# A decoder layer on one core: five row buffers, single part buffers, larger DMA pieces and a new order

## The chip, the cores and the metric

The kernel runs on one core of a Trainium2 chip. The metric is the device time of one execution in microseconds; lower is better. Before the change, three runs gave 1161.72, 1155.21 and 1157.89 us, so the median is 1157.89 us.

## The reference

The reference is one pre-norm decoder layer on `x` (16 batches, 256 rows, 512 columns, float32) with a context of the same shape. It has three steps, each added to `x`:

```python
x = x + attn(layernorm(x), q_w, q_b, k_w, k_b, v_w, v_b, o_w, o_b)   # 16 heads of 32, causal softmax
x = x + xattn(ctx, ctx, layernorm(x), ssm_kernel, D, 8)              # products k*v, long convolution, times q
x = x + ffn(layernorm(x), w_gate_up, w_down)                         # rows and weights rounded to 8 bits, SiLU gate
```

In the second step every pair of channels of a group of 8 is multiplied along the sequence, convolved with a kernel of 512 taps, and multiplied by the normalized `x`. In the third, rows and weights are quantized to 127 levels and scaled back, and the width between is 1408.

## The kernel before, in words

**Two stages.** Until about 622 us on the profile's clock the kernel works on attention, batch by batch; each batch has four units of four heads, 64 units in all. Beside this, GpSimd builds the products of context channels (the "pairs") and stores them in device memory, and the feed-forward weights are quantized. After that come 32 tiles of 128 rows, each with the convolution, the normalization and the feed-forward layer.

**The way of one batch through attention.** `norm_load` (L670) brings 256 rows of `x` into a buffer `xt`. VectorE takes the statistics (L679 to L681), GpSimd the inverse root (`norm_root`, L685), ScalarE writes the normalized rows `xn` (`norm_rows`, L696). For accuracy, rows and weights are each held as a sum of two float16 parts: `turn_hi` (L705, ScalarE) makes `xh`, `turn_lo` (L712, GpSimd) makes the rest `xl`. Two DMA transposes (`turn_out`, L718) turn them into `xhT` and `xlT`, which the query, key and value projections read (`mm3`, L658 to L660: three matmuls for each product). The buffer `xt` is still in use: GpSimd adds the output bias to it (`norm_bias`, L701), and at the end of the batch the output projection is added to it (`out_rows`, L745) and it is stored (`out_store`, L750, twice for each batch). Only then may the buffer take a new batch.

**The way of one unit.** The projections of queries and keys go from PSUM to `qkhl` in two parts each (`project_hi` L766, `project_lo` L771). `project_store` (L778) writes them to device memory, and five DMAs of `project_stack` (L785) read them back, stacked on 96 partitions, as `st`. Then come the scores (L800), the maximum (L809), the exponentials (L816), the inverse sums spread to 32 columns each in `lb` (`scores_spread`, L827, GpSimd), the transposes of the probabilities (L841) and the weighting with the values (`weigh_mm`, L869 to L876). There the inverse sums are transposed too and copied to `lt` (L882), and the result is scaled with them (L887).

**What sets the order.** The order on each engine is fixed before the run by a planner in the kernel's own code (class `Plan`). Every step has an engine, an expected duration, the steps that it follows, the buffers that it takes, and a due time. The planner goes through the steps on a clock of its own; of the steps that are ready and have room in their buffers, it takes the one with the earliest due time. Each engine then runs its instructions in that order, and so does the queue of SyncE (SP), which issues every DMA of the kernel: an instruction that waits holds up all behind it. The due times are formulas in T = 8.8 (the planner's length of a unit), with a table of shifts on top, one row for each kind of step and one column for each stretch of planned time:

```python
pl.add(("xi", b), "SP", t - 9.5 * T, 0.44, norm_load, b, late=1.9, dma=1.5, new=[xt])
...
pl.add(("xp", b), "POOL", t - 8.3 * T, 0.69, norm_root, b, late=0.1, after=[("xs", b, 1)])
...
pl.add(("xh", b), "ACT", t - 7.5 * T, 0.94, turn_hi, b, after=[("xr", b, 0), ("xr", b, 1)], new=[("xh", b)], use=[("xn", b)])
...
s["when"] += v[sum(s["when"] >= b for b in bounds)] if v else 0.0
```

In the planner's keys, `xi` is the load of a batch, `xs` its statistics, `xp` the root, `xc` the shift, `xr` the normalized rows, `xh` and `xl` the two parts, `xo` the two transposes, `qm` the query and key projections, `xb` the bias, `pi` the load of a projection weight.

**The start.** The four projection weights (1 MB each) are loaded (L596), their squares are summed for a scale (`proj_norm`, L603), the scale goes through two small matmuls and a dozen small VectorE instructions (L608 to L639), and the weights are transposed on TensorE (`proj_turn`, L646) and split into two float16 parts (`proj_hi` L649, `proj_lo` L653).

Of the kernel before, what the change touches and what calls it, by code (L numbers as in the profile page):

```python
# [108 lines left out]
def kernel(  # L109
# [16 lines left out]
    P = 128  # L126
# [416 lines left out]
    if True:  # L543
# [50 lines left out]
        def proj_in(nm):  # L594
            wl = wld.tile([P, KC, D], F32, name=f"wl_{nm}")
            nc.sync.dma_start(wl, dict(q=q_w, k=k_w, v=v_w, o=o_w)[nm].rearrange("(o p) i -> p o i", p=P))  # L596
            wraw[nm] = wl
# [17 lines left out]
        def scale_top(j):  # L615
            pt, t2 = tps2[j]
            ti = t2.bitcast(I32)
            nc.vector.tensor_reduce(t2[:, 0:1], pt[:2, :P], op=ALU.max, axis=AX.X)
            nc.vector.tensor_scalar(t2[:, 0:1], t2[:, 0:1], 4.0, 2.0 ** -30, ALU.mult, ALU.max)

            nc.vector.tensor_scalar(ti[:, 1:2], ti[:, 0:1], 1, EXPMASK, ALU.logical_shift_right, ALU.bitwise_and)
            nc.vector.tensor_scalar(t2[:, 2:4], idf[:2, :2], t2[:, 1:2], None, ALU.mult)
# [5 lines left out]
        def scale_all(j):  # L628
# [8 lines left out]
            nc.vector.tensor_tensor(bias[:, j:j + 2, :], bias[:, j:j + 2, :], ap(sc, j, [[1, 2], [0, KC]]), ALU.mult)  # L637
# [9 lines left out]

        def proj_hi(nm, kc):
            nc.scalar.activation(wT[nm][0][:, kc, :], wps[nm, kc], AF.Copy, scale=sc[:, 2, names.index(nm):names.index(nm) + 1])  # L649

        def proj_lo(nm, kc):
            hi, lo = wT[nm]
            nc.vector.scalar_tensor_tensor(  # L653
                lo[:, kc, :], wps.pop((nm, kc)), sc[:, 2, names.index(nm):names.index(nm) + 1], hi[:, kc, :],
                ALU.mult, ALU.subtract)
# [9 lines left out]
        XB, STB = 3, 4  # L665


        def norm_load(b):
            xt = ap2.tile([P, 2, DX], F32, tag="xt", bufs=XB, name=f"xt{b}")
# [33 lines left out]
        def turn_hi(b):  # L703
            xh = ap2.tile([P, 2, D], F16, tag="xh", name=f"xh{b}")
# [4 lines left out]
        def turn_lo(b):  # L709
            xn, xh = xns.pop(b)  # L710
            xl = ap2.tile([P, 2, D], F16, tag="xl", name=f"xl{b}")
# [63 lines left out]
        def project_store(b, g):  # L775
            pjs.pop(("qk", b, g))
            qk_d = dram.tile([4, P, S], F16, tag="qk_d", bufs=4, name=f"qk_d{b}_{g}")
            nc.sync.dma_start(qk_d.rearrange("n p s -> p n s"), qks.pop((b, g)))  # L778
            qkd[b, g] = qk_d

        def project_stack(b, g, n):
            if n == 0:
                stks[b, g] = ap2.tile([96, 2, 4, S], F16, tag="st", bufs=STB, name=f"st{b}_{g}")
            r3, first, n, src = ((0, 0, 2, 1), (1, 0, 1, 1), (1, 1, 1, 3), (2, 0, 1, 0), (2, 1, 1, 2))[n]
            nc.sync.dma_start(  # L785
                stks[b, g][32 * r3:32 * r3 + 32].rearrange("r j h s -> r (j h) s")[:, 4 * first:4 * first + 4 * n, :],
                bass.AP(qkd[b, g].tensor, qkd[b, g].offset + src * P * S, [[S, 32], [32 * S, 4 * n], [1, S]]))


        def scores_mm(b, g, qc, h2):  # L790
# [8 lines left out]
            for hh in range(2):  # L799
                nc.tensor.matmul(  # L800
                    ps[:, hh, :nk], stk[:, 0, 2 * h2 + hh, qc * P:(qc + 1) * P], stk[:, 1, 2 * h2 + hh, :nk],
# [23 lines left out]
        def scores_spread(b, g):  # L825
            lb = ap2.tile([P, 2, P], F32, tag="lb", bufs=2, name=f"lb{b}_{g}")
# [53 lines left out]
        def weigh_sums(b, g):  # L880
            lt = ap2.tile([P, S], F32, tag="lt", name=f"lt{b}_{g}")
# [179 lines left out]
        def weight_scales_out():  # L1061
# [12 lines left out]
        pl = Plan(xt=XB, xn=1, xh=2, xl=2, xhT=2, xlT=2, v=2, pj=2, qk=3, st=STB, s=2, pr=2, lb=2, pt=3, tt=2, av=1,  # L1074
                  lt=2, ah=2, ct=1, cr=2, kT=2, p=2, kv=2, qw=3, qb=2, qt=2, x1=5, q=2, qT=4, sd=1, kv2=3, c=2, u=UB, oT=3, x2=8, xn2=2, xb=2, xq=5, ac=3,
# [5 lines left out]
        for n, nm in enumerate(names):  # L1081
            j = n // 2
            pl.add(("pi", nm), "SP", -80 + 10 * n, 0.55, proj_in, nm, late=1.5, dma=3.3)
# [73 lines left out]
        def batch(b):  # L1157
            t = KC * T * b
            xt = ("xt", b)
            if True:  # L1160
                pl.add(("xi", b), "SP", t - 9.5 * T, 0.44, norm_load, b, late=1.9, dma=1.5, new=[xt])
                if b == 0:
                    pl.add("ob", "SP", -45, 0.5, bias_rows, late=2.0, dma=0.8)
# [117 lines left out]
        for i in range(NT):  # L1281
# [76 lines left out]
        bounds = (60,330,570,680,1010)  # L1358
        shift = {
            ("bi", 2): (0.8, 5.7, 3, 5.9, 1.9, 8.6),  # L1360
            ("bk", 3): (14.4, 12.2, -4.6, 11.1, 15.6, 13.5),
            ("bn", 2): (-4.8, 0.7, 13.6, -2.3, -10.8, 2.5),
            ("bp", 2): (0.2, -9, 3.2, 0, 2.1, 3.1),
            ("bq", 2): (8.5, -3.6, 0.7, 0.7, -24, 0.7),
            ("br", 2): (6.5, 6.7, 1.5, 1.5, -20.1, 1.5),
            ("bs", 2): (0.5, 0.5, 12, 0.5, 20.5, 11.6),
            ("bt", 2): (-3.1, 4.5, 6, 10.4, -3.2, -23.3),
            ("ck", 2): (-1.3, -3.1, -0.1, 0.4, -3.2, -0.3),
            ("cl", 3): (-2.5, 1.1, -0.3, 2.3, -4.4, 1.3),
            ("cm", 2): (-3.9, -1.5, -4.7, -1, -1.5, -4.8),  # L1370
            ("cm", 3): (-3.3, -0.5, 5.2, 4.4, 7.2, -7.4),
            ("co", 2): (-2.8, 5.1, -9.1, 6.1, -12.9, -12.1),
            ("cr", 2): (-4.6, 3.8, -1.4, 0.3, 0.6, 8),
            ("cs", 3): (-7.5, -6, -24.7, -8.3, -15.4, -9.2),
            ("ct", 3): (2, 2.5, 0.3, 0.3, 5.3, -0.5),
            ("cu", 3): (0.2, 1.3, -10.5, -7.1, -6.1, 10.5),
            ("cw", 2): (-1.4, 14, 15.9, -13.5, -1.4, -10.2),
            ("cx", 2): (-27.7, -25.8, -20.3, 0.1, -26.2, -22.6),
            ("cz", 2): (-0.6, 1.6, 0.1, -1.1, 0.1, 0.1),
            ("dm", 2): (9.4, 21.8, 4.5, 11.7, 42.3, 23.4),  # L1380
            ("do", 2): (6.5, -0.8, -1, -6.8, -0.7, -20.7),
            ("dr", 2): (17.3, 17, 7.9, 9, 24.4, 14.2),
            ("ds", 2): (-1.2, -1.7, 7, -1.7, -3.6, 4.7),
            ("fc", 3): (-1.3, 2.5, -6.8, -2.3, 1.7, 1.8),
            ("fd", 2): (-0.3, 0.4, -7.3, 2.9, 0.4, -2.9),
            ("fm", 2): (-14, -14, -17.7, -12.3, -15.4, -10.3),
            ("fm", 3): (1.6, 0.8, -2.2, -0.7, 6.5, 3.9),
            ("fn", 2): (0.2, 0.9, -0.7, 0.2, 2, -4.5),
            ("fo", 2): (2.3, -7.2, 16.2, 3.2, 1.4, -7.2),
            ("fp", 2): (6.6, -2.6, 6.6, -1.9, -11, -3.8),  # L1390
            ("fq", 2): (0.8, -4.2, 0.7, -3, 5.5, 0.8),
            ("fr", 2): (-4.7, 2.6, -0.2, 8.5, 5.7, -28.6),
            ("fs", 2): (-0.1, -20.6, -16.5, 0.2, -23.3, -16.9),
            ("ft", 2): (0.6, 15.2, 12.5, 0.6, 7.1, -0.6),
            ("fv", 2): (1.4, -0, 2.3, -0.3, -8.8, 0.3),
            ("fw", 2): (-1.5, 12.8, 14.2, 14.4, 7.3, 13.3),
            ("gl", 3): (-0.4, 0.4, -0.4, -0.4, -1.3, 0.2),
            ("gm", 4): (0.2, 0.2, 0.4, -2.3, 0.8, -0.2),
            ("gs", 3): (5.5, -5.8, 4.4, 7.8, 8.9, 7.6),
            ("gu", 3): (0.5, 11.3, 16.5, 10.1, 0.5, 24.4),  # L1400
            ("om", 4): (1.9, -9, 5.4, 5.1, -0.8, 3.8),
            ("or", 3): (2.2, 12.8, -4, -0.4, -4, 2.9),
            ("os", 3): (-2.5, 6.4, 18.1, 4, 7.2, 14.8),
            ("pa", 2): (-0.2, 2.1, 1.2, -0.2, -0.2, 2.1),
            ("pb", 2): (8.6, -0.4, 4.8, 4.8, 5.7, 5.9),
            ("pc", 2): (-20.3, -17.7, 4.8, 0.4, 3.9, 4.8),
# [93 lines left out]
```

## Time and profile before

| | before |
|---|---|
| median of 3 runs | 1157.89 us (1155.21 to 1161.72) |
| the profiled execution | 1164.23 us, span 1162.4 us, mean granted TensorE clock 0.993 |
| TensorE busy | 1076.4 us (93%) |
| VectorE busy | 1015.8 us (87%) |
| GpSimd busy | 947.5 us (82%) |
| ScalarE busy | 838.0 us (72%) |
| DMA | 229.48 MB in 269026 packets, mean 197 GB/s |

All durations below come from the one profiled execution. A line such as L670 is a line of the kernel. A wait in the tables is idle time of the engine named first, put down to whatever released it last. SPq is the queue of SyncE. In the rows by window, each engine's busy time is followed by the number of its instructions, then come the granted TensorE clock (1.00 is full speed), the busy share of the 16 DMA engines, and GB/s.

### The profile page before, as it was taken

What the parts mean: (1) busy time and instruction counts of PE and PEld (TensorE: products, weight loads), DVE (VectorE), ACT (ScalarE), POOL (GpSimd) and SP (SyncE); (2) the same over time, 40 slices, a digit from 0 to 9 for tenths busy, and PEclk for the clock granted to TensorE, in tenths of its full rate; (3) what the DMA queues carried; (4) which work ended last, traced back from release to release, by engine and by line L of the source; (5) the groups of instructions that cost most, each with busy time, mean ns of one, the idle gap of its engine ahead of it and who ended that gap; (6) DMA issues with size and microseconds to landing.
All of it is one profiled execution on the core that took longest, in us unless ns stands there. A gap on an engine that the chain in (4) does not pass through costs nothing.

```text
span 1162.4 us, 25593 instructions
## 1 busy us (share of the span) xinstructions
PE 1076.4 (93%) x8503; PEld 766.8 (66%) x8503; DVE 1015.8 (87%) x3188; ACT 838.0 (72%) x1999; POOL 947.5 (82%) x924
## 2 busy tenths in 40 slices
PE   4999889999999989999999889999999999999965
PEld 3766657776667756776666666767767667766632
DVE  5999678888788877987787999999999999999997
ACT  6898878898998878998885456575556566655444
POOL 4497888889999966899514799999999999999962
PEclk9999999999999999999999999999999999999989
DMA  7687798888888977879548956657666766676422
GB/s 244 166 226 246 207 225 219 246 262 229 229 245 233 264 215 199 251 228 258 172 145 274 280 153 189 186 148 192 168 175 169 186 167 168 174 187 156 102 48 66
DMA packets 269026, 229.48 MB, mean 197 GB/s; under 512 B 125177, under 2 KB 223519, under 8 KB 268767
## 3 DMA queue, kind: packets, MB, share of 16 engines
q1 hardware_dynamic: 268895, 227.85, 70.4%
q8 instruction: 67, 1.10, 0.4%
q14 instruction: 64, 0.52, 0.1%
HBM read 124.10 MB, written 75.74 MB: 172 GB/s over the span
## 4 chain that ended last, share of the span: by engine, by line
DVE 32%; PE 31%; POOL 13%; ACT 9%; DMA 8%; issue 5%; SPq 2%; DVEq 0%; POOLq 0%; ACTq 0%
DVE hp L450 4%; PE g L425 4%; ACT p L816 3%; DVE s L454 3%; DVE u L338 3%; DVE p L809 3%; PE pj_qk L659 3%; PE pj_qk L658 3%; PE pj_qk L660 3%; DMA xlT<-xl 2%; DVE u L341 2%; PE c L324 2%; PE c L326 2%; PE c L325 2%; POOL g L443 2%
## 5 line engine op out<-in xcount | busy, mean ns | idle before, releaser
L816 ACT ACTIVATE p<-p,nmax 128x256 f32<-128x256 f32 (+1 forms) x512 | 230.0, 454 | 11.3 <-DVE nmax L809 10.7
L809 DVE CUSTOM_DVE_ANT_0 p<-s,mask,esc 128x128 f32<-128x128 f32 (+1 forms) x512 | 187.1, 411 | 14.8 <-PE s L800 14.6
L324 PE MATMUL c<-bkv,T 128*128 128x288 f16 x640 | 183.2, 286 | 9.4 <-issue 3.2
L325 PE MATMUL c<-bkv,T 128*128 128x288 f16 x640 | 183.1, 286 | 0.0
L326 PE MATMUL c<-bkv,T 128*128 128x288 f16 x640 | 183.0, 286 | 0.0
L425 PE MATMUL g<-w,xq 128*128 128x384 bf16 (+1 forms) x1024 | 169.1, 315 | 13.1 <-DVE o L528 6.3
L964 POOL TENSOR_TENSOR kv<-p,kv 128x1152 f16<-128x1152 f32 x64 | 152.0, 2382 | 7.9 <-ACT kv L959 7.8
L946 POOL TENSOR_TENSOR p<-kT 128x1024 f32<-128x1024 f32 x64 | 143.9, 2249 | 2.3
L425 PEld LDWEIGHTS <-xq 128*128 128x128 bf16 x1024 | 100.4, 98 | 68.0 <-issue 8.1
L443 POOL TENSOR_TENSOR g<-g,sw 128x704 f32<-128x704 f32 x60 | 101.0, 1705 | 3.9 <-ACT g L436 3.9
L816 ACT ACTIVATION_READ_ACCUMULATOR p<-p,nmax 128x1 f32 x512 | 100.4, 196 | 0.0
L800 PE MATMUL s<-st 96*128 96x128 f16 (+1 forms) x512 | 84.5, 247 | 8.9 <-DVE nmax L809 8.4
L338 DVE TENSOR_TENSOR u<-c,qT 128x512 f32<-128x512 f32 x128 | 87.3, 682 | 5.9 <-PE c L326 5.3
L766 ACT ACTIVATE qkhl<-pj_qk,bias 128x256 f16<-128x256 f32 x128 | 59.8, 469 | 45.3 <-PE pj_qk L660 33.7
L771 DVE SCALAR_TENSOR_TENSOR qkhl<-pj_qk,bias,qkhl 128x256 f16<-128x256 f32 x128 | 59.9, 478 | 33.5 <-ACT qkhl L766 21.0
L827 POOL TENSOR_SCALAR lb<-lsum 128x256 f32<-128x256 f32 x64 | 26.0, 406 | 75.6 <-DVE lsum L823 48.9
L357 POOL TENSOR_TENSOR u<-u 128x512 f32<-128x512 f32 x60 | 76.9, 1282 | 9.6 <-DVE u L338 9.6
L510 PE MATMUL d<-w,hq 128*128 128x512 bf16 x352 | 80.9, 379 | 3.8 <-DVE hp L450 3.0
L324 PEld LDWEIGHTS <-T 128*128 128x128 f16 x640 | 62.6, 98 | 29.1 <-DVE u L344 5.9
L659 PE MATMUL pj_qk<-xlT,wq_hi 128*128 128x256 f16 x256 | 70.5, 275 | 10.7 <-DMA xlT<-xl 10.7
L841 PE MATMUL pt<-idf,p 128*128 128x128 f32 x524 | 79.9, 275 | 0.0
L658 PE MATMUL pj_qk<-xhT,wk_hi 128*128 128x256 f16 x256 | 70.0, 273 | 7.3 <-ACT qkhl L766 6.9
(236 smaller groups left out, 3326.1 us busy)
## 6 DMA issues: line engine op xcount, KB each, us to landing
kv_d<-kv SPq DMA_DIRECT2D x64, 576.0 KB, 3.5
bkv<-kv_d SPq DMA_DIRECT2D x64, 576.0 KB, 3.9
qk_d<-qkhl SPq DMA_DIRECT2D x64, 256.0 KB, 2.9
st<-qk_d SPq DMA_DIRECT2D x256, 64.0 KB, 2.7
T<-pad_d SPq DMA_DIRECT2D x64, 256.0 KB, 4.2
x_d<-xt SPq DMA_DIRECT2D x32, 256.5 KB, 3.5
bx<-x_d SPq DMA_DIRECT2D x32, 256.5 KB, 3.6
xt<-in_x_dram SPq DMA_DIRECT2D x16, 512.0 KB, 4.2
```

Source lines behind the costliest of these rows:

```text
L324: nc.tensor.matmul(reg, T[:, 0, d:d + P], kv[:, mi, 0, :], start=mi == 0, stop=False)
L325: nc.tensor.matmul(reg, T[:, 0, d:d + P], kv[:, mi, 1, :], start=False, stop=False)
L326: nc.tensor.matmul(reg, T[:, 1, d:d + P], kv[:, mi, 0, :], start=False, stop=mi == li)
L338: nc.vector.tensor_tensor(ap(u, uo, [[UW, 2], [64, 4], [1, 64]]), ap(pc, 0, [[512, 2], [64, 4], [1, 64]]), ap(qT, qo, [[96, 2], [8, 4], [1 ...
L425: nc.tensor.matmul(pg[:, :c.stop - c.start].rearrange("p (r o) -> p r o", o=P), t["xq"][:, kc, :], w1[:, (o + c.start) // P:(o + c.stop) / ...
L443: (nc.gpsimd if i < NT - 2 else nc.vector).tensor_tensor(ts[i]["g1"][:, c], ts[i]["g1"][:, c], sw1[:, I + c.start:I + c.stop], ALU.mult)
L658: nc.tensor.matmul(ps, lh, rh, start=first, stop=False)
L659: nc.tensor.matmul(ps, lh, rl, start=False, stop=False)
L809: nc.vector.tensor_tensor_reduce(out=prs[b, g][qc][:, h, :], in0=ps[:, hh, :nk], in1=mask2[:, P - qc * P:2 * P], op0=ALU.add, op1=ALU.min, ...
L816: nc.scalar.activation(pr[:, h, :], pr[:, h, :], AF.Exp, scale=-1.0, bias=nmax[:, qc, h:h + 1], accum_out=lsum[:, qc, h:h + 1])
L946: nc.gpsimd.tensor_tensor(ap(p, 0, [[NKV, 4], [64, 4], [1, 64]]), ap(kT, o, [[96, 4], [0, 4], [1, 64]]), ap(kT, o, [[96, 4], [8, 4], [1, 6 ...
L964: nc.gpsimd.tensor_tensor(kv[:, :, 1, :], p, kv[:, :, 0, :], ALU.subtract)
```

## The change

It has five parts.

- The rows of a batch (`xt`) get five buffers in place of three, each a little narrower.
- The two float16 parts `xh` and `xl`, the spread inverse sums `lb` and their transposed copy `lt` get one buffer in place of two.
- Larger pieces: the projection weights are read so that a partition gets four whole consecutive rows (8 KB together) and not four rows that lie apart (2 KB each). The transposed columns then come out in another sequence, and `cols` puts them back as the two parts are written. The queries and keys are stored as 2 KB for each partition in place of four pieces of 512 B, and `st` has its axes swapped, so that one of the five reads moves pieces of 1 KB; the other four keep 512 B.
- Two small VectorE instructions of the scale become a `scalar_tensor_tensor`.
- The order: the load of the output weight may come only after the second transpose of batch 0, two planned durations differ, and every row of the table of shifts is new, with eight columns in place of six.

```diff
-            nc.sync.dma_start(wl, dict(q=q_w, k=k_w, v=v_w, o=o_w)[nm].rearrange("(o p) i -> p o i", p=P))
+            nc.sync.dma_start(wl, dict(q=q_w, k=k_w, v=v_w, o=o_w)[nm].rearrange("(p o) i -> p o i", p=P))
...
-            nc.vector.tensor_scalar(t2[:, 2:4], idf[:2, :2], t2[:, 1:2], None, ALU.mult)
+            nc.vector.scalar_tensor_tensor(t2[:, 2:4], idf[:2, :2], 1.0, ap(t2, 1, [[0, 2]]), ALU.mult, ALU.mult)
...
-            nc.vector.tensor_tensor(bias[:, j:j + 2, :], bias[:, j:j + 2, :], ap(sc, j, [[1, 2], [0, KC]]), ALU.mult)
+            nc.vector.scalar_tensor_tensor(bias[:, j:j + 2, :], bias[:, j:j + 2, :], 1.0, ap(sc, j, [[1, 2], [0, KC]]), ALU.mult, ALU.mult)
...
+        def cols(t):
+            return t.rearrange("k (p o) -> k o p", o=KC)
+
         def proj_hi(nm, kc):
-            nc.scalar.activation(wT[nm][0][:, kc, :], wps[nm, kc], AF.Copy, scale=sc[:, 2, names.index(nm):names.index(nm) + 1])
+            nc.scalar.activation(cols(wT[nm][0][:, kc, :]), wps[nm, kc].rearrange("k (o p) -> k o p", o=KC), AF.Copy,
+                                 scale=sc[:, 2, names.index(nm):names.index(nm) + 1])
...
-        XB, STB = 3, 4
+        XB, STB = 5, 4
...
-            xt = ap2.tile([P, 2, DX], F32, tag="xt", bufs=XB, name=f"xt{b}")
+            xt = ap2.tile([P, 2, D + 4], F32, tag="xt", bufs=XB, name=f"xt{b}")
...
-            xh = ap2.tile([P, 2, D], F16, tag="xh", name=f"xh{b}")
+            xh = ap2.tile([P, 2, D], F16, tag="xh", bufs=1, name=f"xh{b}")
...
-            xl = ap2.tile([P, 2, D], F16, tag="xl", name=f"xl{b}")
+            xl = ap2.tile([P, 2, D], F16, tag="xl", bufs=1, name=f"xl{b}")
...
-            qk_d = dram.tile([4, P, S], F16, tag="qk_d", bufs=4, name=f"qk_d{b}_{g}")
-            nc.sync.dma_start(qk_d.rearrange("n p s -> p n s"), qks.pop((b, g)))
+            qk_d = dram.tile([P, 4, S], F16, tag="qk_d", bufs=4, name=f"qk_d{b}_{g}")
+            nc.sync.dma_start(qk_d, qks.pop((b, g)))
...
-                stks[b, g] = ap2.tile([96, 2, 4, S], F16, tag="st", bufs=STB, name=f"st{b}_{g}")
-            r3, first, n, src = ((0, 0, 2, 1), (1, 0, 1, 1), (1, 1, 1, 3), (2, 0, 1, 0), (2, 1, 1, 2))[n]
+                stks[b, g] = ap2.tile([96, 4, 2, S], F16, tag="st", bufs=STB, name=f"st{b}_{g}")
+            r3, j, w, src = ((0, 0, 2, 1), (1, 0, 1, 1), (1, 1, 1, 3), (2, 0, 1, 0), (2, 1, 1, 2))[n]
             nc.sync.dma_start(
-                stks[b, g][32 * r3:32 * r3 + 32].rearrange("r j h s -> r (j h) s")[:, 4 * first:4 * first + 4 * n, :],
-                bass.AP(qkd[b, g].tensor, qkd[b, g].offset + src * P * S, [[S, 32], [32 * S, 4 * n], [1, S]]))
+                stks[b, g][32 * r3:32 * r3 + 32].rearrange("r h j s -> r h (j s)")[:, :, j * S:(j + w) * S],
+                bass.AP(qkd[b, g].tensor, qkd[b, g].offset + src * S, [[4 * S, 32], [32 * 4 * S, 4], [1, w * S]]))
...
-            lb = ap2.tile([P, 2, P], F32, tag="lb", bufs=2, name=f"lb{b}_{g}")
+            lb = ap2.tile([P, 2, P], F32, tag="lb", bufs=1, name=f"lb{b}_{g}")
...
-            lt = ap2.tile([P, S], F32, tag="lt", name=f"lt{b}_{g}")
+            lt = ap2.tile([P, S], F32, tag="lt", bufs=1, name=f"lt{b}_{g}")
...
-            pl.add(("pi", nm), "SP", -80 + 10 * n, 0.55, proj_in, nm, late=1.5, dma=3.3)
+            pl.add(("pi", nm), "SP", -80 + 10 * n, 0.55, proj_in, nm, late=1.5, dma=2.9, then=[("xo", 0, 1)] * (n == 3))
...
-                    pl.add("ob", "SP", -45, 0.5, bias_rows, late=2.0, dma=0.8)
+                    pl.add("ob", "SP", -45, 2.0, bias_rows, late=2.0, dma=0.8)
...
-        bounds = (60,330,570,680,1010)
+        bounds = (-50,10,60,330,570,680,1010)
...
-            ("qm", 3): (0, 1.9, -1.6, -1.4, -1.6, -1.4),
+            ("qm", 3): (1, -6.6, 5.6, 2.5, -4.1, 4.8, 6.6, -4.6),
...
-            ("xh", 2): (1, -0.1, -0.1, -0.1, 32.8, 1),
+            ("xh", 2): (47.7, 33.2, 30.1, 31.9, 36.7, 30.1, 35, 2.8),
-            ("xi", 2): (-29.5, 8.3, 8.2, -18.2, 5.6, -45.6),
+            ("xi", 2): (0, -12.5, 1, 5.4, 8.4, 4.4, -4.3, 6.3),
...
-            ("xo", 3): (-36.7, -30.1, 24.9, -48.9, -48.1, -40.2),
-            ("xp", 2): (-3.4, 1.4, -4, -3.5, -14.8, -3.3),
+            ("xo", 3): (-1.3, 9.6, -0.7, -20.2, -2.7, 0.3, 4.7, 9.5),
+            ("xp", 2): (37.9, 32.2, 44.8, 31.9, -0.9, 38.6, 34.4, 31.5),
...
```

The table has about ninety such rows; the ones shown are those of a batch's way to its projections.

## Prediction before the run

> **What bounds the kernel now.** I read the page's totals first, then busy time by window, then who waited for whom, and last the timeline around the longest of those waits. The totals, and the attention stage in four windows (the columns are named with the profile above):
>
> ```profile
> span 1162.4 us, 25593 instructions
> PE 1076.4 (93%) x8503; PEld 766.8 (66%) x8503; DVE 1015.8 (87%) x3188; ACT 838.0 (72%) x1999; POOL 947.5 (82%) x924
> ...
> 25.00:60.00 35.00, 33.36 (x279) 26.38 (x278) 31.32 (x117) 28.65 (x72) 16.19 (x15) 1.00 0.58 151
> 60.00:330.00 270.00, 253.70 (x2208) 183.59 (x2206) 227.61 (x871) 236.93 (x716) 236.70 (x191) 0.99 0.82 231
> 330.00:570.00 240.00, 224.82 (x1953) 161.70 (x1952) 193.48 (x752) 210.42 (x624) 210.09 (x167) 0.99 0.83 235
> 570.00:622.00 52.00, 49.61 (x451) 34.68 (x449) 43.45 (x166) 42.63 (x152) 7.15 (x13) 1.00 0.60 188
> ```
>
> TensorE carries attention: 561.5 of 597 us busy, so 35.5 us is the most that any order can win there. From 680 to 1100 us TensorE and VectorE are both above 95% busy; an edit before that moves this stage as a whole. What TensorE waited for in 60 to 620 us (total, times, longest), and two waits of the SP queue:
>
> ```profile
> PE pj_qk L659 <- DMA xlT<-xl: 10.7, 6, 3.7
> PE s L800 <- DVE nmax L809: 7.2, 16, 1.7
> PE pj_qk L658 <- ACT qkhl L766: 6.9, 9, 1.1
> ...
> SPq L785 <- DMA qk_d<-qkhl: 72.4, 41, 4.8
> ...
> SPq L670 <- DMA x_d<-xt: 21.0, 8, 6.2
> ```
>
> The first place is the late transpose of `xl`. The SP queue shows why: the load of `xt` waits for the store of the batch three before it. One case, from store to stall:
>
> ```profile
> 399.47 0.35 SPq L750 DMA_DIRECT2D x_d<-xt  x1
> ...
> 404.34 0.40 SPq L670 DMA_DIRECT2D xt<-in_x_dram  x1
> ...
> 423.06 1.32 SPq L718 DMA_TRANSPOSE xlT<-xl  x1
> ...
> 429.26 0.37 PE L659 MATMUL pj_qk<-xlT,wq_hi 128*128 128x256 f16 x1 [3.44 <-DMA xlT<-xl]
> ```
>
> Store, 4.9 us, load, 18.7 us, transpose, 6.2 us, matmul. All thirteen loads from batch 3 on are issued 2.9 to 6.6 us after a second store of the batch three before (108.08 after 104.19, 132.70 after 127.97, 180.07 after 175.91, and so on). The stall also costs clock (the granted clock is the third number from the right):
>
> ```profile
> 428.00:430.00 2.00, 0.74 (x4) 0.54 (x4) 1.76 (x2) 0.00 (x0) 0.00 (x0) 0.74 1.14 361
> 430.00:432.00 2.00, 2.00 (x12) 1.54 (x11) 0.17 (x2) 0.20 (x1) 0.00 (x0) 0.50 0.73 273
> 432.00:434.00 2.00, 2.00 (x18) 1.79 (x18) 0.73 (x2) 2.00 (x4) 0.00 (x0) 0.91 0.67 250
> ```
>
> The missing clock is (0.26 + 0.50 + 0.09) x 2 = 1.7 us. The stall at 161.73 (3.67 us) has 0.68, 0.50 and 0.97 behind it: 1.7 us too.
>
> **The change part by part.**
>
> *Five row buffers.* The load of batch b then waits for the store of batch b-5, two batches or about 70 us earlier, so the 18.7 us from load to transpose no longer follow a store. This takes away TensorE's 10.7 us and the 3.4 us of clock: -14.1 us. What is late next is `xh` and `xl` themselves if the order asks for them late (below). The load adds nothing to SP (0.38 us each, as many as before); SP also loses the 21.0 us for which all DMAs behind a blocked load stood still. Ends: 0 and, with what that freed queue gives the later waits, -18.
>
> *Single part buffers.* Here the Trainium skill ("Trainium Kernel Development and Optimization", Best Practices) speaks against the change: it says to double-buffer so that transfers lie beside computing. By that rule four rings lose their overlap. The trace: `xh` and `xl` are written 1.04 and 2.13 us long and are free once the transposes land, 3.9 and 3.5 us after issue; from batch 2 on the next batch's transposes come 26 us or more later. `lt` is read to its end at least 2.9 us before its next copy. Only `lb` is held: in this trace 12 of its 63 successors are written before the transposes at L869 have read the one before (taken as done 0.9 us before the copy at L882 starts), by 30.6 us together. But 1.0 us of this lies before 430 us, 4.1 us in the stall just shown, 0.5 us near 475, 9.6 us at 507 to 540 us, where GpSimd is full, and the other 15.4 us after 565 us, where it has little else to do. Its pairs end with the store at 572 us and are first read at 603.8 us: 30 us of cover. If that cover were gone, the 9.6 us would come on the path, and `xl`, queued behind a waiting `lb` on GpSimd, would hold TensorE. By the rule +10, by the trace 0; I take 0.
>
> *Larger pieces.* The skill's "DMA: Bandwidth & Descriptors" (Specifications) calls 512 B enough for full line rate, so pieces of 512 B and 2 KB have nothing to win: 0 us. The trace is less kind to small pieces: in 5 to 10 us, weights and rows in 2 KB pieces move 363 GB/s at a share of 0.99, while the window 140 to 160 us, with many 512 B and transposed pieces, moves 217 GB/s at 1.00. Yet what can be won is small: a store of 256 KB in 512 B pieces lands in 2.9 us, one of 576 KB in pieces of over 4 KB in 3.5 us, a read of 128 KB in 2.9 us and one of 64 KB in 2.7 us. At an estimated 0.3 us for each of 64 stores and 64 larger reads, SP and DMA win some 38 us in sum, but TensorE waited for `st` only 0.4 us in all. The scores are far behind their reads. I take 0 (-4 to +1). The axes of `st` change no matmul.
>
> *The start.* Of the first 25 us TensorE is busy 8.9. The chain goes weight q landing at 8.45, squares (1.91), rows and part of batch 0 (1.5 + 1.04), squares of k to 14.9, scale to 18.4, parts and transposes, first projection at 25.36. The k weight landed near 12.6, just when ScalarE came free, so faster pieces alone win at most 0.3 us; the new order can win the 2.5 us of rows on ScalarE. Moving the output weight's load (1 MB, issue 1.97 us) behind the second transpose (issued 16.25) spares it and costs nothing: its squares start at 25.33, its transposes at 36.3. The strided writes of 32 ScalarE and VectorE instructions (0.67 and 0.75 us) are not shown anywhere; the nearest row, the copy at L933 that writes in rows of 64, takes 0.577 us against 0.581 for a plain one, so 0, at worst doubled on the eight that stand before the first projection: +4. The two `scalar_tensor_tensor` are 0.22 and 0.17 us now; beside GpSimd a VectorE addition of one element a row (L981) took 1.68 us, so -1 to +2. I take -1 for the start (-3 to +5).
>
> *The rest of the order.* Every due time is new, so waits of 7.2 + 6.9 us and the losses between the stages (620 to 680 us: TensorE 7.7, VectorE 8.0 us idle) and in the last 60 us are dealt anew. Nothing in the trace gives a sign; 0, from -18 (half of these and the tail's) to +20.
>
> Sum: -14.1 - 1 = -15 us, that is 1149 against this execution's 1164.2 (span and 1.8 us around it). That execution lies 6.3 us above the median of the runs, so I set the sum against the median: 1157.9 - 15 = 1143 us.
>
> **The rivals.**
>
> *The idle time only moves.* Without the wait for `xlT`, TensorE meets the maximum (L809) or the parts of `qkhl` a little later: these two already cost 14.1 us, most of them under 1 us. For it: ScalarE is 88% busy in 60 to 570 us. Against: the two long stalls, 7.1 us and all of the lost clock, belong to no other engine. Then only some 3 us remain: 1155.
>
> *The new order also gathers the rest.* Idle time of 35.5 falls to 10, with the clock 3.4, the start 3, the transition 3: -35, 1123. For it: three columns of the table shape the time before 60 on the planner's clock, in place of one. Against: no order keeps TensorE at 98% with four engines above 80%.
>
> *The new order brings the wait back (slower).* The table puts the root (`xp`) and the part `xh` back by 30 to 48, while the projections (`qm`) move by at most 10. On the planner's scale `xh` was due 66 us ahead of its batch and is now due about 35; the projections are due about 30 ahead. Between lie `xh`, `xl`, a transpose and its landing: 1.04 + 2.13 + 1.3 + 3.5 = 8 us. If that chain slips as it did at 423 us, every batch stalls and not two. With 3.5 us of idle and 1.7 us of clock at every second of 13 batches, 34 us stand against the 14 won: +20, 1178. It decides from 1.1 us a batch on. Against: due times are only ranks among steps that are ready, and the rows now lie in SBUF long before.
>
> *The change doesn't do what it says:* five buffers do nothing if the planner still plans with three. It is given the same constant, `xt=XB`, so I leave this out.
>
> **How the numbers follow.** About 0.5% (5.8 us) is what a measurement of this kernel can tell from no change. The main forecast, 1132 to 1152, gets 0.48; the large gain 0.16; the idle time that moves 0.14, all of it within 0.5%; the slower case 0.22. So faster 0.64, same 0.14, slower 0.22. The range 1120 to 1168 leaves out the best third of the large gain and the worse half of the slow case.
>
> **What would show it.** Right: no wait of L670 on `x_d`, TensorE's wait for `xlT` under 2 us, no granted clock below 0.95 in 100 to 560 us, attention over near 607 us in place of 622, and 620 to the end as long as before. Wrong: a wait for `xlT` in most batches (slow rival); a first projection after 27 us (strided writes); GpSimd waiting before L827 with pairs stored after 595 us (`lb`); or a conv stage longer by over 6 us.

## The result, and the profile after

The kernel after takes 1165.02 us (median of 6 runs, 1163.77 to 1165.61), the one before 1158.47 us (6 runs): a ratio of 1.0055, with a 95% interval of 1.0035 to 1.0075. So it is 6.5 us slower, where 15 us faster was forecast. The profiled execution after took 1165.3 us. Lines of code lie 5 further down than before (L675 loads rows, L723 transposes, L791 reads `st`, L806 scores, L815 maximum). The totals, the start and the attention stage in the windows of before (start and end in us, length, busy time of TensorE, its weight loads, VectorE, ScalarE and GpSimd with counts, granted clock, DMA share, GB/s):

```profile
span 1163.5 us, 25635 instructions
PE 1077.3 (93%) x8503; PEld 765.7 (66%) x8503; DVE 1021.1 (88%) x3188; ACT 846.1 (73%) x1999; POOL 948.1 (81%) x924
...
0.00:25.00 25.00, 6.72 (x27) 5.16 (x28) 14.99 (x44) 16.13 (x17) 9.46 (x15) 1.00 0.88 304
25.00:60.00 35.00, 28.45 (x206) 21.33 (x205) 32.20 (x91) 30.46 (x58) 10.94 (x7) 1.00 0.44 119
60.00:330.00 270.00, 252.97 (x2192) 182.54 (x2191) 223.57 (x869) 237.46 (x703) 242.38 (x196) 0.98 0.82 232
330.00:570.00 240.00, 231.43 (x2044) 168.19 (x2042) 203.17 (x788) 214.65 (x658) 191.71 (x155) 1.00 0.79 229
570.00:622.00 52.00, 50.62 (x442) 34.85 (x440) 39.35 (x156) 43.29 (x144) 25.89 (x25) 1.00 0.59 191
```

TensorE does the same work. Up to 60 us it has done 35.2 us of it, where before it had done 42.3; from 330 to 570 us it does 6.6 us more. In these two traces the two cancel: the first matmul of the convolution starts at 621.75 and at 621.58 us. But the profiled execution of before took 6.3 us more than the median of its runs, so the two traces alone cannot show the loss; in a second trace of before (e13 below) that matmul starts at 617.55 us. What TensorE waited for in 60 to 620 us, and two waits of the SP queue in 25 to 622 us:

```profile
PE s L806 <- DVE nmax L815: 11.9, 14, 3.3
PE pj_qk L663 <- DVE qkhl L776: 8.9, 10, 1.6
PE av L875 <- DVE al L900: 1.1, 2, 0.7
...
SPq L791 <- DMA qk_d<-qkhl: 40.6, 27, 4.3
...
SPq L675 <- DMA x_d<-xt: 7.3, 4, 3.5
```

The wait for `xlT`, 10.7 us before, is gone, and the loads of rows wait 7.3 us for the store in place of 21.0. But the three largest waits are 21.9 us where they were 24.8: the wait for the maximum is 4.7 us longer and that for the parts of queries and keys 2.0 us, so over half of the 10.7 us has moved there. One stall is new:

```profile
86.74 1.15 ACT L965 CAST kv<-p 128x1152 f16<-128x1152 f32 x1 [3.67 <-DMA kv_d<-kv]
...
89.25 0.59 PE L806 MATMUL s<-st 96*128 96x256 f16 x2 [3.31 <-DVE nmax L815]
...
88.00:90.00 2.00, 0.75 (x4) 0.56 (x4) 1.50 (x8) 2.00 (x4) 2.00 (x1) 0.61 1.31 237
90.00:92.00 2.00, 2.00 (x12) 1.38 (x10) 1.90 (x9) 2.00 (x7) 2.00 (x3) 0.50 1.13 149
92.00:94.00 2.00, 2.00 (x11) 1.44 (x10) 1.15 (x6) 1.94 (x8) 1.35 (x2) 0.50 1.57 277
94.00:96.00 2.00, 2.00 (x15) 1.54 (x14) 0.00 (x0) 1.04 (x5) 0.00 (x0) 0.69 0.72 197
```

ScalarE stands 3.67 us for a store of `kv` (products of the pairs), issued at 78.01 and landed 8.7 us later, with four loads of 256 KB issued just ahead of it; TensorE stands 3.31 us for the maximum behind it, and its clock then loses (0.39 + 0.50 + 0.50 + 0.31) x 2 = 3.4 us.

### The profile page after: what moved, and what is told of

It is laid out like the page before. It is cut to its first block, busy times and chain, and to the rows that moved or that the text cites. A ratio compares the mean times of both kernels' runs of the same rounds, so it can differ in the third digit from the quotient of the medians.

```text
span 1163.5 us, 25635 instructions
## 1 busy us (share of the span) xinstructions
PE 1077.3 (93%) x8503; PEld 765.7 (66%) x8503; DVE 1021.1 (88%) x3188; ACT 846.1 (73%) x1999; POOL 948.1 (81%) x924
## 4 chain that ended last, share of the span: by engine, by line
PE 42%; DVE 29%; ACT 9%; POOL 7%; DMA 7%; issue 4%; SPq 1%; DVEq 0%; ACTq 0%; POOLq 0%
PE g L425 6%; PE c L324 3%; PE c L326 3%; PE c L325 3%; DVE hp L450 3%; ACT p L822 3%; DVE s L454 3%; PE pj_qk L663 3%; DVE p L815 2%; PE pj_qk L665 2%; PE pj_qk L664 2%; DVE u L338 2%; PE s L806 2%; DVE u L341 2%; PE pt L847 2%
## 5 line engine op out<-in xcount | busy, mean ns | idle before, releaser
L815 DVE CUSTOM_DVE_ANT_0 p<-s,mask,esc 128x256 f32<-128x256 f32 (+1 forms) x512 | 187.2, 410 | 17.9 <-PE s L806 17.6
L806 PE MATMUL s<-st 96*128 96x256 f16 (+1 forms) x512 | 84.6, 247 | 13.8 <-DVE nmax L815 13.6
L965 ACT CAST kv<-p 128x1152 f16<-128x1152 f32 x64 | 73.5, 1148 | 6.8 <-DMA kv_d<-kv 5.2
L806 PEld LDWEIGHTS <-st 96*128 96x128 f16 x512 | 46.3, 98 | 45.0 <-issue 26.6
```

The lines of the kernel that those rows point to most:

```text
L806: nc.tensor.matmul(ps[:, hh, :nk], stk[:, 2 * h2 + hh, 0, qc * P:(qc + 1) * P], stk[:, 2 * h2 + hh, 1, :nk], start=True, stop=True)
L815: nc.vector.tensor_tensor_reduce(out=prs[b, g][qc][:, h, :], in0=ps[:, hh, :nk], in1=mask2[:, P - qc * P:2 * P], op0=ALU.add, op1=ALU.min, ...
```

## The experiments

Each is timed against the kernel before on the same chip, and chips and sessions differ a little, so the ratio counts and not the median. A ring is the set of buffers that a tile goes through in turn. The measure of scatter is the kernel before against itself (e13): 1.0012, interval 0.9988 to 1.0036.

| run | what | median us | ratio to before, 95% |
|---|---|---|---|
| after | the change | 1165.02 | 1.0055 (1.0035 to 1.0075) |
| e1 | after, plain weight writes | 1158.49 | 0.9999 (0.9984 to 1.0014) |
| e2 | after, old forms of two operations | 1162.68 | 1.0040 (1.0023 to 1.0058) |
| e3 | before, wide weights | 1165.92 | 1.0063 (1.0046 to 1.0080) |
| e4 | before, five rows, single parts | 1168.17 | 1.0081 (1.0058 to 1.0104) |
| e5 | before, four rows, single `xh`, `xl` | 1157.44 | 0.9997 (0.9979 to 1.0016) |
| e6 | before, three rows, single parts | 1169.20 | 1.0089 (1.0059 to 1.0120) |
| e7 | before, new order | 1205.57 | 1.0403 (1.0370 to 1.0436) |
| e8 | e1 and e2 together | 1157.44 | 0.9999 (0.9985 to 1.0014) |
| e9 | after, small `qk_d` pieces | 1164.34 | 1.0051 (1.0033 to 1.0069) |
| e10 | e8, `ct` loaded sooner | 1156.47 | 0.9976 (0.9964 to 0.9988) |
| e11 | e8, wide weights, strided reads | 1156.89 | 0.9985 (0.9971 to 0.9998) |
| e12 | e8, wide weights, strided transposes | 1157.53 | 0.9985 (0.9969 to 1.0001) |
| e13 | before, again | 1161.11 | 1.0012 (0.9988 to 1.0036) |
| e14 | e8, sum of rows later | 1159.39 | 1.0005 (0.9988 to 1.0023) |
| e15 | e10, e11, e14 and one move more | 1157.88 | 0.9995 (0.9977 to 1.0014) |
| e16 | e10 and e11 | 1156.34 | 0.9963 (0.9949 to 0.9977) |

**The strided writes: e1 and e3.** e1 takes the weight pieces out of after, e3 puts them alone into before.

```diff
-            nc.sync.dma_start(wl, ...[nm].rearrange("(p o) i -> p o i", p=P))
+            nc.sync.dma_start(wl, ...[nm].rearrange("(o p) i -> p o i", p=P))
...
-            nc.scalar.activation(cols(wT[nm][0][:, kc, :]), wps[nm, kc].rearrange("k (o p) -> k o p", o=KC), AF.Copy, ...)
+            nc.scalar.activation(wT[nm][0][:, kc, :], wps[nm, kc], AF.Copy, ...)
...
-                cols(lo[:, kc, :]), wps.pop((nm, kc)).rearrange("k (o p) -> k o p", o=KC), ..., cols(hi[:, kc, :]), ...)
+                lo[:, kc, :], wps.pop((nm, kc)), ..., hi[:, kc, :], ...)
```

> The kernel after, but with the weights read in 2 KB lines and written by proj_hi and proj_lo without strides, as before; its order is kept. Theory A, the start pays: a strided write takes 1.40 us on ScalarE and 1.36 us on VectorE in place of 0.69 and 0.75, 16 times on each; what lies ahead of the first projections (8 of the 16, 5 to 6 us of VectorE) is on the path, so the kernel is 5 to 8 us faster than after, 1157 to 1160 us, and the first projection starts near 24 us in place of 27.4. Theory B, the order pays: what the start loses is made up by idle time of the attention stage whatever it is, and the time stays within 2 us of after (1163 to 1167).

> The kernel before with the weights alone in 8 KB lines, and so the strided writes of proj_hi and proj_lo; its order is kept. Theory A: the mirror of the first run, 5 to 8 us slower than before, 1163 to 1166 us. Theory B: idle time later takes it in, within 2 us of before (1156 to 1160).

Removing them from after wins all of the 6.5 us; adding them to before costs as much. The groups of instructions up to 45 us (busy us, mean ns) of before, then of after:

```profile
L649 ACT ACTIVATE wq_hi<-wq,sc 128x512 f16<-128x512 f32 x3 | 2.0, 675 | 0.0
...
L653 DVE SCALAR_TENSOR_TENSOR wq_lo<-wq,sc,wq_hi 128x512 f16<-128x512 f32 x3 | 2.2, 748 | 1.5 <-ACT wq_hi L649 1.5
```

```profile
L653 ACT ACTIVATE wq_hi<-wq,sc 128x512 f16<-128x512 f32 x3 | 4.2, 1406 | 2.1 <-DVE sc L634 1.2 <-PE wq L646 0.9
L658 DVE SCALAR_TENSOR_TENSOR wq_lo<-wq,sc,wq_hi 128x512 f16<-128x512 f32 x3 | 4.1, 1358 | 0.0
```

On ScalarE only the target differs: 2-byte values written 8 bytes apart. VectorE also reads `wq_hi` 8 bytes apart, so what its write alone costs is not shown. In e1 the first projection starts at 25.93 us in place of 27.43 (24 had been expected), which is 1.5 us; the rest is won after it, where most of the keys, the values and the output weights are still split. TensorE's 25 to 60 us in e1:

```profile
25.00:60.00 35.00, 32.87 (x265) 26.53 (x269) 31.13 (x115) 27.56 (x69) 15.78 (x13) 1.00 0.57 160
```

That is 4.4 us more than the 28.45 of after, the 1.5 us included; where the last 2 us are won was not traced. Theory B (idle time takes the loss in) has fallen. Both runs change the size of the pieces too; e11 below keeps the large pieces without the strided writes and is as fast as with small ones, so the writes are the cause.

**The two rewritten operations: e2, and e14 later.**

```diff
-            nc.vector.scalar_tensor_tensor(t2[:, 2:4], idf[:2, :2], 1.0, ap(t2, 1, [[0, 2]]), ALU.mult, ALU.mult)
+            nc.vector.tensor_scalar(t2[:, 2:4], idf[:2, :2], t2[:, 1:2], None, ALU.mult)
...
-            nc.vector.scalar_tensor_tensor(bias[:, j:j + 2, :], ..., 1.0, ap(sc, j, [[1, 2], [0, KC]]), ALU.mult, ALU.mult)
+            nc.vector.tensor_tensor(bias[:, j:j + 2, :], ..., ap(sc, j, [[1, 2], [0, KC]]), ALU.mult)
```

> The kernel after, with the two operations of scale_top and scale_spread back in their old forms (tensor_scalar and tensor_tensor). Theory A: in after each of the two first ones stands 1.2 us longer than its own work because GpSimd is busy beside it; tensor_scalar has one tensor as input and should not be held (0.2 us in place of 1.38), tensor_tensor has two and is held as well, so 1 us is won and the time is 1164. Rival: both old forms are free, 2.4 us are won (1162.5); or both are held, nothing is won.

The time is 2.3 us lower, close to the 2.4 of the rival with free forms. But this is luck: the intervals of e2 and after overlap, the first projection starts no sooner (27.52 against 27.43 us), and the trace says that the form is not it. VectorE and GpSimd of e2 (start, duration):

```profile
15.11 1.38 DVE L622 TENSOR_SCALAR t<-idf,t 2x2 f32<-2x2 f32 x1
...
17.91 0.15 DVE L635 TENSOR_SCALAR sc<-sc 128x1 f32<-128x1 f32 x1
18.10 1.37 DVE L637 TENSOR_TENSOR bias<-bias,sc 128x8 f32<-128x8 f32 x1
...
14.34 2.13 POOL L717 TENSOR_TENSOR xl<-xn,xh 128x1024 f16<-128x1024 f32 x1 [5.97 <-ACT xh L710]
...
17.09 2.35 POOL L706 TENSOR_TENSOR xt<-xt,ob 128x1024 f32<-128x1024 f32 x1
```

Both old forms last as long as the new ones (1.38 and 1.37 us), and both end when GpSimd's instruction ends (16.47 and 19.44). So theory A's free `tensor_scalar` was wrong, and what remains is that both are held. The operations between them on one element a row with one tensor as input, like L635, take their 0.15 us beside the same GpSimd instruction. e14 moves only GpSimd's sum, in the plain start of e8:

```diff
+            some = [s for s in plan if s["key"] == ("xb", 0)]    # behind ("xp", 3) on GpSimd
```

> The plain start (1157.44 us), with GpSimd's sum of the rows of batch 0 with the bias (2.35 us) moved behind four later steps of GpSimd. It stood beside the last operation of VectorE's chain of scales, which took 1.36 us there and 0.17 us in before. Theory: that operation is held until GpSimd's ends, and with the sum gone it takes 0.2 us, 1.2 us are won, 1156.3. Rival: the operation's own work or form takes the time, and it stays at 1.36 us.

The operation at L637 fell from 1.36 to 0.17 us with its form unchanged, so GpSimd's place beside it was the cause:

```profile
18.53 0.17 DVE L637 TENSOR_TENSOR bias<-bias,sc 128x8 f32<-128x8 f32 x1
```

The first projection started at 24.67 in place of 25.84 us, but the whole shows no gain (1.0005 against e8's 0.9999): the 1.2 us that were expected lie within the two intervals.

**Row buffers and single parts: e4, e5, e6.** All in the order of before, instruction for instruction.

```diff
-        XB, STB = 3, 4
+        XB, STB = 5, 4        # e4; e5: 4; e6: 3
...
+            xh ... bufs=1, xl ... bufs=1     # e4, e5, e6
+            lb ... bufs=1, lt ... bufs=1     # e4 and e6 only
...
+        pl = Plan(xt=3, ...      # e4 and e5: the planner still counts three
```

> The kernel before with five row buffers and single xh, xl, lb and lt; the planner still counts as before, so the order is the very same. The prediction's own term: the waits of TensorE for xlT and the clock lost after them go, -14 us, 1144 us. Theory A (they go, and about that much is won in the middle of after as well): 1142 to 1150. Rival, the idle time moves to the next wait: 1153 to 1158. Rival, single buffers hold up GpSimd or ScalarE in an order that was made for two: slower than before.

> The kernel before, its own order, with four row buffers and single xh and xl; lb and lt stay double. The run before it (five rows, single xh, xl, lb and lt in the old order) was 9.6 us slower than before, with GpSimd standing 10.5 us at one lb. Theory L, the single lb did that: here the load of rows no longer waits for the store of x_d, and the kernel is as fast as before or up to 6 us faster (1152 to 1159). Theory X, the single xh and xl or the further rows did it: 1162 to 1168 again.

> The kernel before, its own order and three row buffers, with single xh, xl, lb and lt. Theory L: the single lb holds up GpSimd in an order made for two, and the time is that of the five-row run, 1164 to 1170. If five row buffers by themselves win the 14 us of the prediction, this run is 14 us slower than the five-row run (1182); if they win nothing here, the two agree within 3 us.

Theory L holds. With single `lb` and `lt` the old order is about 10 us slower, whether with five rows (e4) or with three (e6); without them (e5) it is as fast as before. Five rows against three, all else equal, are worth the difference of 1.0081 and 1.0089: 1 us, and by the two intervals not over some 5. Waits in e6 in 60 to 622 us, and the last of them in e13 (before):

```profile
POOL lb L827 <- PE av L869: 29.4, 6, 9.7
POOL lb L827 <- DVE nmax L809: 13.0, 2, 8.2
...
ACT kv L959 <- POOL p L950: 12.1, 10, 4.2
```

```profile
ACT kv L959 <- POOL p L950: 2.8, 8, 0.8
```

Neither of the first two waits is there in before; but GpSimd waited at L827 for other things then, 61.2 us in all in e13 against 74.5 in e6, so the single rings add 13 us. What stands behind on its queue comes later: ScalarE waits 9 us more for the pairs `p`, and from 330 to 570 us TensorE does 218.9 us of work against 225.6 in e13. TensorE's wait for `xlT` does not grow (7.7 against 7.3). The waits stand at `lb`; `lt` was not made double by itself.

And e5 shows why the rows win nothing. Its loads never wait for the store of `x_d`, but TensorE's waits for `xlT` are still there:

```profile
PE pj_qk L659 <- DMA xlT<-xl: 6.4, 4, 2.9
```

They were 10.7 in the profile of before and are 7.3 in e13. (e5 has single `xh` and `xl` too; of these its trace shows one wait, 0.8 us of ScalarE for the transpose of `xh`.) The same batch as in the prediction, in e13 (before) and in e5:

```profile
401.08 0.40 SPq L670 DMA_DIRECT2D xt<-in_x_dram  x1
...
416.30 2.14 POOL L712 TENSOR_TENSOR xl<-xn,xh 128x1024 f16<-128x1024 f32 x1
...
419.80 1.24 SPq L718 DMA_TRANSPOSE xlT<-xl  x1
...
425.57 0.37 PE L659 MATMUL pj_qk<-xlT,wq_hi 128*128 128x256 f16 x1 [2.60 <-DMA xlT<-xl]
```

```profile
400.13 0.44 SPq L670 DMA_DIRECT2D xt<-in_x_dram  x1
...
414.91 2.16 POOL L712 TENSOR_TENSOR xl<-xn,xh 128x1024 f16<-128x1024 f32 x1
...
418.56 1.30 SPq L718 DMA_TRANSPOSE xlT<-xl  x1
...
424.57 0.35 PE L659 MATMUL pj_qk<-xlT,wq_hi 128*128 128x256 f16 x1 [2.90 <-DMA xlT<-xl]
```

From load to transpose it is 18.7 us in the one and 18.4 in the other: each step stands in its place in the order, behind the work of other batches, and in before the transpose of `xl`, ready at 421.29, was issued at 423.06 behind its twin and a load of weights. The load's wait for the store ran beside this.

**The order alone: e7.**

```diff
-        bounds = (60,330,570,680,1010)
+        bounds = (-50,10,60,330,570,680,1010)        # with the table of after; rings as before
```

> The kernel before with all of its buffers and pieces, in an order planned with the new table of shifts, the new bounds and the two new entries, and rings as before. Theory T, the table was found for the rings of after and is worth nothing with other rings: 1165 to 1185 us. Theory U, the order is what wins the 20 us that after makes up between 60 and 570 us: 1150 or less.

Theory T, and beyond its range: 47 us slower. This table does harm with other rings than those for which it was found. The other way round, after with four or three row buffers in its own order cannot run, since its steps would wait for each other for ever; double `lb` and `lt` together do not fit into SBUF beside five rows. Not tried was a planner that is told of a fourth row buffer and keeps the old table.

**Pieces of queries and keys: e9.**

```diff
-            qk_d = dram.tile([P, 4, S], F16, tag="qk_d", bufs=4, ...)
+            qk_d = dram.tile([4, P, S], F16, tag="qk_d", bufs=4, ...)      # and st as before
```

> The kernel after, with queries and keys stored and read in 512-byte pieces as before, its order kept. The prediction's term was 0 (-4 to +1): the read of the keys lands 0.3 us sooner and few waits of TensorE hang on it. Theory: within 2 us of after, 1163 to 1167. Rival: the middle of after, which wins some 20 us between 60 and 570 us, needs the sooner landing, and the time is 1170 or more.

1.0051 against 1.0055: no difference.

**The plain start, and ways to keep the wide pieces: e8, e11, e12.**

```diff
 e11: reads PSUM across, writes without a stride
+            nc.scalar.activation(wT...rearrange("k (p o) -> k p o", o=KC), wps[nm, kc].rearrange("k (o p) -> k p o", o=KC), ...)
 e12: TensorE writes PSUM across
+                nc.tensor.transpose(wps[nm, kc].rearrange("k (p o) -> k o p", o=KC)[:, oc, :], wraw[nm][:, oc, ...], idf)
```

> The kernel after with both parts of its start undone: the weights in 2 KB lines with plain writes, and the two operations of the scales in their old forms. The first was worth 6.5 us by itself and the second 2.3 us. If they add up, 1156 us, 2 us faster than before; if the second lies in the shadow of the first, 1158.5.

> The plain start again, but with the weights in 8 KB lines, put back in order by the reads: proj_hi and proj_lo read PSUM with a stride of 512 bytes between neighbours and write without one. If only the strided write of 2-byte values costs (1.40 and 1.36 us against 0.69 and 0.75), both take what they took before, and the time is that of the plain start or 1 us less for the sooner loads, 1156 to 1158. If any stride costs as much, 1162 to 1164.

> The same with the order put back by TensorE: each transpose of a weight tile writes PSUM with a stride of 16 bytes, and proj_hi and proj_lo stay as before. If TensorE's writes to PSUM take no longer for the stride, 1156 to 1158; if they take twice as long, the 64 transposes cost some 0.11 us each more, of which the 32 ahead of the first projection are on the path, 1159 to 1161.

e8 is as fast as before and as e1, so the old forms add nothing to the plain writes. Neither e11 nor e12 pays for its stride. First the parts in e11, then the transposes in e12 and, last, in before:

```profile
L656 ACT ACTIVATE wq_hi<-wq,sc 128x512 f16<-128x512 f32 x3 | 2.1, 687 | 2.6 <-PE wq L646 1.5 <-DVE sc L634 1.2
...
L661 DVE SCALAR_TENSOR_TENSOR wq_lo<-wq,sc,wq_hi 128x512 f16<-128x512 f32 x3 | 2.2, 741 | 0.0
```

```profile
L646 PE MATMUL wq<-idf,wl_q 128*128 128x128 f32 x12 | 3.3, 428 | 9.3 <-DMA wl_q<-in_L_attn_q_w_dram 4.7 <-DVE wq_lo L653 4.5
```

```profile
L646 PE MATMUL wq<-idf,wl_q 128*128 128x128 f32 x12 | 3.3, 428 | 6.4 <-DMA wl_q<-in_L_attn_q_w_dram 3.5 <-DVE wq_lo L653 3.0
```

Read with a stride of 512 bytes from PSUM, the parts take 687 and 741 ns, as without one; a transpose written 16 bytes apart takes 428 ns, as before (ends of matmuls are modelled, but the starts agree: two groups of four follow each other by 0.88 us in both). What the wide pieces win themselves is 1.6 us by the ratios (0.9985 against 0.9999), within the two intervals.

**The pocket at 76 to 100 us: e10, e15, e16.** The order of e10 differs from that of e8 only in the place of four loads; e16 is e10 with the reads of e11; e15 has two moves more.

```diff
+            # all of ("cl", 8, 0..3) directly behind ("cr", 3)                         e10, e15, e16
+            # ("xb", 0) behind ("xp", 3); state_parts behind ("xs", 9, 1), its store later    e15
```

> The kernel of the run with the plain start (1157.44 us), with one edit of the order: the four loads of the second group of pairs (ct, 256 KB each) are issued ahead of the five reads of st before them, near 63 us in place of 67.6 to 70.7. There TensorE lost 7.5 of the 40 us from 60 to 100, because ScalarE stood 2.5 us for a store of kv that had these loads ahead of it in the queues. Theory S, a pocket of one transfer: it goes, and 3 to 6 us are won, 1151 to 1154. Rival, the pocket moves: the reads of st come 2 us later and TensorE waits for them instead, 1156 to 1160.

> The kernel after with the weights in 8 KB lines put in order by strided reads, the scales in their old forms, and the second group of pairs loaded ahead of the five reads of st; nothing else. Alone, the reads gave a ratio of 0.9985 to before and the loads 0.9976. If they add up, 0.996, some 1154 us; if the pocket's idle time only moves, 0.998 to 0.999, as in the run of all edits.

> All edits together on the kernel after: weights in 8 KB lines put in order by strided reads, the scales in their old forms, the second group of pairs loaded sooner, GpSimd's sum of the rows of batch 0 later, and the 5 us that VectorE works on the state's kernel at 90 us moved to where its result is still early (330 us). The strided reads gave 0.5 us against the plain start, the loads 2 us; the moved sum is worth 1.2 us and the state's work the 2 us that TensorE waited for VectorE at 93 to 97 us with the clock after it. If they add up, 1151 to 1154 us; if idle time moves on as it did with the row buffers, 1155 to 1157.

(A pocket is a short stretch in which one late transfer leaves several engines idle.) e10 wins 2.7 us on e8 by the ratios, a little less than the 3 to 6 expected. (Its median falls into the range of the rival, but the waits for `st` that the rival forecast did not come.) ScalarE's wait for the store of `kv` falls from 2.54 to 1.04 us, and TensorE's wait for the maximum behind it from 2.19 to 0.67. With the reads it is 0.9963, as the sum of the two gains: 4.3 us faster than before and, by the ratios, 10.7 us faster than after, the fastest kernel of this study. e15 missed both of its forecasts. It has less idle time in its pocket, but in 200 to 330 us TensorE loses 3.6 us that e16 doesn't lose (e15 above, e16 below):

```profile
60.00:100.00 40.00, 35.33 (x318) 26.29 (x316) 32.80 (x130) 35.83 (x100) 37.86 (x32) 1.00 0.88 218
...
200.00:330.00 130.00, 121.46 (x1073) 87.26 (x1073) 111.78 (x432) 118.94 (x364) 117.20 (x93) 1.00 0.78 233
```

```profile
60.00:100.00 40.00, 34.07 (x293) 25.05 (x292) 34.49 (x124) 35.18 (x98) 36.66 (x30) 1.00 0.95 218
...
200.00:330.00 130.00, 125.06 (x1103) 90.33 (x1102) 111.22 (x436) 120.50 (x368) 118.54 (x95) 1.00 0.79 234
```

VectorE's work on the state's kernel, 5 us, was put at 330 us by the planner's clock; which of the moves opens the new gap was not taken apart.

**The kernel before, again: e13.**

> The kernel before, unchanged, once more with a profile. If the waits for xlT (10.7 us in the profile that the prediction used) are part of each execution, they are there again, 8 to 11 us, whatever its time. If they make the difference between that execution (1164 us) and the median (1158), an execution near the median has 5 us or less of them.

Inconclusive: it took 1163.67 us, again above the median, and its waits for `xlT` were 7.3 us, between the two cases.

## Why the prediction was wrong

*What bounds the kernel:* right. TensorE is busy 1076 to 1077 us in before, after and e16, and what differs is idle time in the attention stage and its start.

*Five row buffers, -14.1 us:* this step failed. The wait for `xlT` did go in after, but not by the buffers alone: e5 takes the load's wait for the store away and leaves 6.4 us of waits for `xlT`; five rows against three are worth 1 us. The prediction took the chain store, load, transpose, matmul for cause and effect because the lines followed each other in time. It did not ask what stood ahead of each step on its own queue. In after the loads come 57 us ahead of the transposes (375.09 and 431.69 for batch 12) where they came 18.7; that is the order's work, for which the five buffers only make room. Even so, TensorE is busy 535.0 us in 60 to 622 us, where it was 528.1 in the profile of before, 531.2 in e13 and 533.4 in e5: 2 to 7 us were to be had, not 14. The rest is the rival "the idle time only moves", as the waits above show.

*Against the median:* the saving was read from an execution 6.3 us above the median and subtracted from the median. Part of the 10.7 us may belong to that execution (7.3 in e13); this stays open.

*Single part buffers, 0:* wrong in the old order, where they cost 10 us, the figure that the rule of double buffers gave. Single `xh` and `xl` are free there, as worked out; single `lb` and `lt` are not. The prediction counted how late each `lb` would come and found cover for it, but GpSimd's queue stands still meanwhile, and the pairs behind it come late; `xl`, which it feared for, does not. In the new order GpSimd waits only 8.4 + 5.7 us for these transposes in 25 to 622 us, and ScalarE 2.6 us for the transpose of `xh`; what that costs is not separable, but e8 as a whole equals before. The predicted sign, pairs stored after 595 us, was there (the last at 601.66), without harm to the convolution.

*Larger pieces, 0:* right for queries and keys (e9), and within 1.6 us for the weights themselves (e11, e12).

*The start, -1 (-3 to +5):* the second step that failed, and the one that made the kernel slower. The strided writes, put at 0, cost 6.5 us by e1 and 7.3 by e3. Two things were wrong. The nearest row, L933, writes in runs of 64 values and says nothing of single values 8 bytes apart. And "at worst doubled on the eight before the first projection" left out the other 24 instructions: only 1.5 us lie before the first projection, the other 5 us behind it. The sign named for it, a first projection after 27 us, came true (27.43). The Trainium skill has a rule that should have been weighed here: "Vector Engine (DVE) Microarchitecture Reference", Measured stream behaviour on trn2, says that a port keeps its rate only for runs of at least two adjacent 4-byte words and gives 1.71 to 2.51 ns a column for a target that hops at every element, 1.05 for one that doesn't. By it, as an estimate, 512 columns cost 0.34 to 0.75 us more; VectorE's 748 to 1358 ns is 0.61, though with 2-byte values and with an input that hops too. That ScalarE pays as well (675 to 1406 ns) the runs alone show. Nor did the rest of the start win its 1 us: with plain writes (e8) TensorE has done 39.8 us of work at 60 us, 2.5 less than before.

*The two operations, -1 to +2:* they took 2.4 us more, a little above the upper end, but not by their form: the old ones were held as long (e2).

*The rest of the order, 0:* about right as a sum. The new order, with five rows, makes good the 10 us that single `lb` and `lt` cost the old one, and opens the pocket at 76 to 100 us, of which 2.7 us could be taken back by moving four loads.

*The slow rival* (the wait for `xlT` comes back) did not happen. The result was slower by a cost that stood in the text only as a bound of the start. From -15 to +6.5 us are 21.5; the 14.1 us of the rows and the 6.5 + 1 of the start make them up.

## What to carry to other kernels

Before a wait in the profile is promised as a gain, take away what is held to cause it with nothing else changed: two instructions that follow each other in time are not yet cause and effect, and the queue between them may set both. When a layout trick makes transfers larger, look at the engine that puts the values back in order, and choose the side on which it hops: here strided reads from PSUM were free, and with strided 2-byte writes each instruction took twice as long. A ring made single can cost through the queue that stands at it, even where its own data have time.

## What the runs showed of the hardware that was not expected

- A float16 write with a step of 8 bytes from one value to the next: 1406 ns against 675 on ScalarE, 1358 against 748 on VectorE (there with one float16 input read alike), for 128x512. Reads from PSUM 512 bytes apart: 687 and 741 ns. Transposes by TensorE into PSUM 16 bytes apart: 428 ns, as without.
- A VectorE multiplication of 2x2 values takes 1.38 us beside a GpSimd instruction, until that instruction ends, and 0.22 us without one; operations with one tensor input of one value a row keep their 0.15 us beside the same instruction, while in before an addition with two tensor inputs of one value a row (L981) took 1.68 us beside another. The Trainium skill ("SBUF — State Buffer", SBUF: two separate sides) calls this an exclusive lock for the whole instruction, and for VectorE operations with two inputs from SBUF or in a two-port mode alone; the runs agree, in that the older form with a single tensor input was held too.
- A store of 576 KB landed in 8.7 us where four loads of 256 KB had been issued ahead of it, against a median of 3.6 us in after; behind it TensorE stood 3.3 us and 3.4 us of clock were missing. With the loads issued sooner (e10 against e8) ScalarE's wait for the store fell from 2.54 to 1.04 us.
